# A two-stream ConvLSTM on one core: the gate product of the even pixels on GpSimd, the residual on VectorE, one row's normalisation on ScalarE

## The chip, the core and the metric

The kernel runs on one core of a Trainium2 chip. The number that counts is the device time of one execution in microseconds; the kernel before has a median of 2023.89 us over three runs (2023.4 to 2026.16). Engines are named as in the profile: PE is TensorE (its weight loads are PEld), DVE is VectorE, ACT is ScalarE, POOL is GpSimd, SP is the engine that issues the DMAs.

## What is computed

`x` is 8 images of 96 channels, 128 rows and 128 columns, float32. It is normalised in 32 groups of channels, then a recurrent cell runs down the rows, and its hidden state is added to `x`:

```python
def step(carry, row_in):                      # one row of all 8 images
    h, c = carry
    ss = conv1d(h, W_ss, padding=1)           # 96 -> 384 channels, 3 taps along the row
    gates = ss + row_in                       # row_in: 1x3 masked convolution of the normalised row
    f, i, o = (sigmoid(part) for part in ...) # each 96 channels
    g = tanh(...)
    c_new = f * c + i * g
    h_new = o * tanh(c_new)
    return (h_new, c_new), h_new
_, hs = lax.scan(step, (h0, c0), rows_of(conv(group_norm(x), W_is * mask)))
return x + hs
```

The scan has 128 steps, and each needs the hidden row of the one before.

## The kernel before

**Two streams.** The images are split in two groups of four, `s = 0` and `s = 1`. Each has its own recurrence, and the kernel alternates between them: a *half-step* n is one row of one group (`row, s = divmod(n, 2)`), 256 half-steps in all. While one group's gates are worked on by ACT and DVE, PE makes the products of the other.

**A fast convolution.** The columns are split in even and odd pixels (`t = 0` and `t = 1`, 256 columns each for four images). For a half-step the operands are `vs` (sum of the even and odd hidden pixels), `vf` (their difference) and `vd` (two shifted differences), and the same three kinds of the normalised input in `xs` for the channels that have 128 partitions free. `hx` holds the hidden row on partitions 0 to 95 and 32 normalised input channels on partitions 96 to 127. Each of the three output tiles A, B and C (one PSUM bank each: A holds the gate f, B the gate i, C the gate o, and a third of g each) gets these products, by the letters that the kernel uses:

- `P`, `Q`, `E`: the input alone (`xs`), one product each, with a `+` in the order for the next half-step;
- `1` (from `vs`) and `2` (from `vf`), into halves 0 and 1 of the bank; then `cp` (ACT copies half 0 to SBUF and adds the bias, line 508), `lo` (DVE, line 512: half 0 = copy + half 1) and `hi` (DVE, line 516: half 1 = copy - half 1);
- `0` and `3` (from `vd`), added to halves 0 and 1 afterwards, which completes the gates.

**Two row halves on PE.** Every product of 128 rows is cut into two of 64 rows, one on the upper and one on the lower half of the PE array (`Lanes`, line 372), and the halves are handed out alternately, so that two products run side by side. A half-step has 3 x 3 input products and 3 x 4 x 2 halves of the others, 33 products; each shows as two weight loads and two matmuls in the profile. Two products into the same bank from different row halves may not run at once: `mm` (line 432) puts a wait ahead of such a product, for the last product into that bank on the other half.

**The order** is written out by hand in `PERIOD` (line 678), a string of about 80 names that is emitted for each half-step n from 2 on, for all engines at once; each engine then runs its own instructions in that order, and a semaphore wait stands where an operand comes from elsewhere. A `'` means half-step n-1, `''` means n-2, `+` means n+1. Other names of the string: `ta` tanh and `si` sigmoid on ACT (lines 520, 527), `fg` f*c on DVE (532), `gt` i*g on DVE (537), `ce` the new cell (547), `th` its tanh on ACT (552), `ou` the hidden row on DVE (560), `S` the sum `vs` (573) and `F` the difference `vf` (585) on DVE, `D` the `vd` on POOL (589), `re` the residual `x += h` on POOL (607). `a` and `b` behind a name are the even and the odd pixels alone.

**Work on POOL for later rows.** Input rows come in blocks of four (`R = 4`). For the block ahead, POOL normalises one image of 128 partitions into `xw` (`widen`, line 297), makes its total (line 315) and its differences (line 316) into `xs`, and normalises the 32 shared channels of an image straight into `hx` (line 297 too). `W` in the order calls `prepare(n - 1)`, which emits all of one half-step's share; `work(n)` (line 640) lists it, `SHARED` says which image's shared channels belong to which row, and `FIRST` holds the shares of half-steps 0 to 7, which also have to catch up. `normalised` makes `total` wait for the last shared normalisation.

Before the recurrence the statistics of all images are taken while `x` streams in; the last few lines of the kernel finish half-step 255 by image pairs.

Neither `vd` nor the residual may start at will: `shifted` makes POOL wait until DVE is done with `vs` and `vf`, because these two read two SBUF operands.

Of the kernel before, what the change touches and what calls it, by code (L numbers as in the profile page):

```python
# [21 lines left out]
def kernel(  # L22
# [276 lines left out]
    def widen(engine, xw, i, n, s, k, j, lo, step=1):  # L299


        norm(
            engine,
            strided(xw[:, i, :], 0, [(step * (W + 1), n), (J + 1, 2), (1, J)]),
            (x0[:, 0, j] if s == 1 and k == lo == 0 else xr[s][:, j, lo * W : (lo + n) * W])
            .rearrange("p (r j t) -> p r t j", r=n, t=2),
            0,
            1,
            s * BH + j,
        )  # L310

    def combine(xw, n, total, differences):

        e, o = xw[:, 0:n, 0:J], xw[:, 0:n, J + 1 :]
        nc.gpsimd.tensor_add(total, e, o)  # L315
        nc.gpsimd.tensor_sub(  # L316
            differences,
            strided(xw[:, 0, :], 0, [(W + 1, n), (J, 2), (1, J)]),
            strided(xw[:, 0, :], J + 1, [(W + 1, n), (0, 2), (1, J)]),
        )  # L320

# [16 lines left out]
    normalised = {}  # L338

    def normalise_shared(engine, s, k, j, lo, hi):  # L340

        normalised[s, k] = norm(
# [61 lines left out]

    lanes = Lanes()
    whole = slice(0, P)

    class HalfStep:


        def __init__(self, n):
            self.n, (self.row, self.s) = n, divmod(n, NH)
            self.ps, self.m1, self.moving, self.done, self.gates, self.th = {}, {}, {}, set(), None, None
            self.started, self.images, self.halves, self.writer = set(), {}, {}, {}
            self.hx = hx[self.s][self.row // R % 2][:, self.row % R]
            self.xs = xs[self.s][self.row // R % 2][:, self.row % R]
            self.c = cs[self.s].rearrange("p t b j -> p (t b j)")
# [105 lines left out]
        def sigmoid(self, a):  # L523
            if self.row == 0 and a == 0:
                return
            gate = self.ps[a][0:C]
            nc.scalar.activation(gate, gate, AF.Sigmoid)  # L527
# [6 lines left out]
        def gated(self, lo=0, hi=BH, t=None):  # L534
            to = self.g if self.row > 0 else self.c
            to, i, g = (self.part(ap, lo, hi, t) for ap in (to, self.ps[1][0:C], self.g))
            nc.vector.tensor_mul(to, i, g)  # L537
# [33 lines left out]
        def total(self, engine=nc.vector, lo=0, hi=BH):  # L571
            e, o = self.pair(lo, hi)
            self.last = engine.tensor_add(self.operand("vs")[:, 0, lo:hi], e, o)  # L573
            row, s = divmod(self.n + 1, NH)
            if engine is nc.vector and row >= R and row % R < 2 and (s, row // R) in normalised:
                tc.add_manual_dep(
                    self.last.ins,
                    normalised[s, row // R].ins.name,
                    mybir.DependencyInfo(mybir.DependencyClass.Sync, mybir.DependencyReason.DATA),
                    reason="the next difference finds the next rows of x normalised",  # L580
                )
# [5 lines left out]
        def shifted(self, lo=0, hi=BH):  # L587
# [6 lines left out]
            if self.last.ins.engine != E.Pool:  # L594
                tc.add_manual_dep(
                    diff.ins,
                    self.last.ins.name,
                    mybir.DependencyInfo(
                        mybir.DependencyClass.Sync, mybir.DependencyReason.SCHED_ONLY
                    ),  # L600
                    reason="GpSimd starts when VectorE is done with both SBUF reads",
                )

        def residual(self):
            s, row = self.s, self.row
            xo = xt[s, row // R][0:C, :, row % R, :].rearrange("p b (j t) -> p t b j", t=2)
            (nc.gpsimd if 2 * row + s < last else nc.vector).tensor_add(xo, xo, self.h)  # L607
# [12 lines left out]
    def own(s, *images):  # L620
        return [(own_image, s, 1, j) for j in images]

    def shared(s, k, *images):
        return [
            (normalise_shared, nc.gpsimd, s, k, *(j if isinstance(j, tuple) else (j, 0, R)))
            for j in images
        ]

    FIRST = [
        own(0, 0),  # L630
        own(0, 1),
        own(0, 2) + shared(0, 1, 0, 1),
        own(0, 3) + [(load_rows, 0, 2)] + shared(0, 1, 2, 3),
        own(1, 0, 1),
        own(1, 2) + shared(1, 1, 0, 1),
        own(1, 3) + [(load_rows, 1, 2)] + shared(1, 1, 2, 3),
        [(own_image, 0, 2, 0), (own_image, 1, 2, 0)],
    ]

    def work(n):  # L640
# [4 lines left out]
        parts = []  # L645
        if r == R - 1 and k + 2 < NB:
            parts.append((own_image, s, k + 2, 0))
        elif r < R - 1 and k + 1 < NB:
            parts.append((own_image, s, k + 1, r + 1))
        if k + 1 < NB:  # L650
            parts += shared(s, k + 1, *SHARED[r])
        if r == R - 2 and k + 2 < NB:
            parts.append((load_rows, s, k + 2))
        return parts

    worked = set()

    def prepare(n):
        if n not in worked:
            worked.add(n)  # L660
            for part, *args in work(n):
                part(*args)

    def finish(n):
# [338 lines left out]
```

## Time and profile before

| | |
|---|---|
| median of three runs | 2023.89 us (2023.4, 2023.89, 2026.16) |
| the profiled execution | 2027.04 us, its span 2025.2 us, clock 0.997 |
| first `fg` of the hand-written order (line 532) | starts at 153.75 us |
| one half-step from there on (66 matmuls) | 7.33 us |
| data moved | 183.90 MB read, 50.33 MB written, 116 GB/s over the span |

How to read it. The span is that of the profiled execution; the 1.8 us between it and that execution's time lie outside the trace. After the statistics, the same 7.33 us pattern repeats some 250 times, so one half-step is read closely and multiplied. In the stretch from 300 to 1900 us these were the groups of one half-step apart from the matmuls (mean duration of one, from the groups by shape in that stretch; "per half-step" is the count over 218, the number of half-steps there):

| line | engine, operation | shape | per half-step | mean ns |
|---|---|---|---|---|
| 508 | ACT copy with bias (`cp`) | 128x256 | 3 | 474 |
| 520 | ACT tanh (`ta`) | 32x512 / 32x256 | 2 / 2 | 592 / 369 |
| 527 | ACT sigmoid (`si`) | 96x512 | 3 | 577 |
| 552 | ACT tanh of the cell (`th`) | 96x256 | 2 | 411 |
| 512, 516 | DVE `lo`, `hi` | 128x256 | 3, 3 | 425, 422 |
| 532 | DVE `fg` | 96x512 | 1 | 696 |
| 537, 547, 560 | DVE `gt`, `ce`, `ou` | 96x256 | 2, 2, 2 | 412, 410, 412 |
| 573, 585 | DVE `vs`, `vf` | 128x256 | 1, 1 | 418, 426 |
| 589 | POOL `vd` | 128x512 | 1 | 1041 |
| 607 | POOL residual | 96x512 | 1 | 1298 |
| 297 | POOL `xw` | 128x512 | 1 | 816 |
| 315, 316 | POOL total, differences of the own image | 128x256, 128x512 | 1, 1 | 641, 1068 |
| 297 | POOL shared channels | 32x512 (or 384, 128) | 1 to 2 | 814 (696, 465) |

In that stretch DVE was busy for 1227.2 us of 1600, ACT for 1202.3 and POOL for 1235.2.

### The profile page before, as it was taken

To read this page: it belongs to the slowest core of one execution; us is meant where nothing else is said; L and a number is where in the kernel's file an instruction comes from. 1 tells how busy PE (TensorE), PEld (TensorE's weight loads), DVE (VectorE), ACT (ScalarE), POOL (GpSimd) and SP (SyncE) were. 2 spreads that over 40 slices of the span, in tenths; PEclk is the share of its full clock that TensorE was granted. 3 is DMA by queue.
4 is the path that set the end of the run, shared out by engine and by line. 5 is a ranking of instruction groups with operands and counts; after the bars stand their busy time and mean duration, and the time that the engine had idled before them with its cause. 6 is when DMAs were issued, how large, how long until landed. Compare 5 with 4: busy or idle time off the path is not lost.

```text
span 2025.2 us, 44842 instructions
## 1 busy us (share of the span) xinstructions
PE 1923.3 (95%) x16936; PEld 1831.0 (90%) x16936; DVE 1529.1 (76%) x3996; ACT 1494.9 (74%) x3161; POOL 1473.1 (73%) x1712
## 2 busy tenths in 40 slices
PE   0289999999999999999999999999999999999998
PEld 0178999999999999999999999999999999999997
DVE  5767777777777777777777777777777777777776
ACT  3776777777777777777777777777777777777776
POOL 3348777777777777777777777777777777777752
PEclk9989999999999999999999999999999999999999
DMA  9994333444334334433433443343344333434411
GB/s 374 424 310 100 98 103 91 112 115 104 82 89 113 92 101 115 113 83 82 110 95 95 116 116 95 79 100 96 93 116 116 96 82 96 107 92 106 116 33 32
DMA packets 103382, 237.11 MB, mean 117 GB/s; under 512 B 5952, under 2 KB 8896, under 8 KB 97280
## 3 DMA queue, kind: packets, MB, share of 16 engines
q1 hardware_dynamic: 103168, 234.25, 42.0%
q8 instruction: 135, 2.21, 0.5%
q14 instruction: 79, 0.65, 0.1%
HBM read 183.90 MB, written 50.33 MB: 116 GB/s over the span
## 4 chain that ended last, share of the span: by engine, by line
PE 93%; DMA 4%; ACT 2%; DVE 1%; issue 0%; SPq 0%; POOL 0%; DVEq 0%; POOLq 0%
PE ps L442 92%; DMA piece<-in_x_dram 3%; DMA xs<-in_x_dram 1%; ACT piece L216 1%; PE ps L174 0%; ACT piece L217 0%; DVE bst L876 0%; ACT hx L295 0%; ACT piece L295 0%; DVE hx L560 0%; ACT xs L216 0%; ACT xs L217 0%; SPq L864 0%; PE pv L251 0%; DVE ps L516 0%
## 5 line engine op out<-in xcount | busy, mean ns | idle before, releaser
L442 PE MATMUL ps<-vd,wl 64*128 64x256 f32 (+1 forms) x6096 | 1390.9, 379 | 0.3
L442 PEld LDWEIGHTS ps<-vd,wl 64*128 64x128 f32 (+1 forms) x6096 | 1028.4, 186 | 45.7 <-issue 2.4
L442 PE MATMUL ps<-vs,wm 64*128 64x256 f32 (+1 forms) x3052 | 775.1, 380 | 4.9 <-POOL vs L573 4.4
L442 PE MATMUL ps<-vf,wm 64*128 64x256 f32 (+1 forms) x3052 | 766.3, 377 | 0.0
L527 ACT ACTIVATE ps<-ps 96x512 f32<-96x512 f32 x766 | 441.6, 577 | 356.2 <-PE ps L442 348.1
L442 PE MATMUL ps<-xs,wx 64*128 64x256 f32 x3080 | 637.8, 377 | 11.1 <-POOL xs L315 11.1
L589 POOL TENSOR_TENSOR vd<-hx 128x512 f32<-128x512 f32 x257 | 266.7, 1038 | 388.5 <-PE ps L442 384.8
L442 PEld LDWEIGHTS ps<-xs,wx 64*128 64x128 f32 x3080 | 494.0, 187 | 14.2 <-POOL xs L315 11.6
L520 ACT ACTIVATE g<-ps 32x256 f32<-32x256 f32 (+1 forms) x1021 | 468.6, 482 | 26.7 <-PE ps L442 6.3
L442 PEld LDWEIGHTS ps<-vf,wm 64*128 64x128 f32 (+1 forms) x3052 | 475.4, 187 | 11.0 <-PE ps L442 0.4
L442 PEld LDWEIGHTS ps<-vs,wm 64*128 64x128 f32 (+1 forms) x3052 | 459.6, 186 | 21.6 <-POOL vs L573 5.4
L512 DVE TENSOR_TENSOR ps<-m,ps 128x256 f32<-128x256 f32 x768 | 326.0, 425 | 192.5 <-ACT m L508 182.0
L442 PE MATMUL ps<-xs,wt 64*128 64x256 f32 x1530 | 453.2, 377 | 0.6 <-DVE ps L516 0.6
L508 ACT ACTIVATE m<-ps,wl 128x256 f32<-128x256 f32 x766 | 361.6, 474 | 90.9 <-PE ps L442 84.3
L532 DVE TENSOR_TENSOR ps<-ps,c 96x512 f32<-96x512 f32 x254 | 176.8, 696 | 232.9 <-PE ps L442 226.9
L607 POOL TENSOR_TENSOR x<-x,hx 96x512 f32<-96x512 f32 x255 | 330.8, 1297 | 6.7 <-DVE hx L560 6.7
L516 DVE TENSOR_TENSOR ps<-m,ps 128x256 f32<-128x256 f32 x768 | 300.8, 422 | 1.3 <-PE ps L442 1.2
L442 PEld LDWEIGHTS ps<-xs,wt 64*128 64x128 f32 x1530 | 280.0, 186 | 12.8 <-DVE ps L516 1.0
L316 POOL TENSOR_TENSOR xs<-xw 128x512 f32<-128x512 f32 (+1 forms) x254 | 270.9, 1067 | 0.0
L297 POOL TENSOR_SCALAR hx<-x,rstd,nmr 32x384 f32<-32x384 f32 (+2 forms) x312 | 225.8, 724 | 33.2 <-DMA x<-in_x_dram 1.1
L297 POOL TENSOR_SCALAR xw<-xr,rstd,nmr 128x512 f32<-128x512 f32 x252 | 205.6, 816 | 7.1 <-DVE nmr L289 6.5
L537 DVE TENSOR_TENSOR g<-ps,g 96x256 f32<-96x256 f32 x507 | 189.0, 413 | 3.8 <-ACT g L520 3.8
(91 smaller groups left out, 1223.1 us busy)
## 6 DMA issues: line engine op xcount, KB each, us to landing
xr<-in_x_dram SPq DMA_DIRECT2D x124, 512.0 KB, 6.4
x<-in_x_dram SPq DMA_DIRECT2D x63, 768.0 KB, 6.1
out_dram<-x SPq DMA_DIRECT2D x62, 768.0 KB, 4.6
xs<-in_x_dram SPq DMA_DIRECT2D x30, 1024.0 KB, 12.3
piece<-in_x_dram SPq DMA_DIRECT2D x16, 1024.0 KB, 12.3
x<-in_x_dram SPq DMA_DIRECT2D x62, 256.0 KB, 3.2
xs<-in_x_dram SPq DMA_DIRECT2D x4, 512.0 KB, 8.7
out_dram<-x SPq DMA_DIRECT2D x2, 576.0 KB, 3.7
```

The source lines that it names most:

```text
L297: return engine.tensor_scalar(dst, src, scale, shift, ALU.mult, ALU.add)
L316: nc.gpsimd.tensor_sub(differences, strided(xw[:, 0, :], 0, [(W + 1, n), (J, 2), (1, J)]), strided(xw[:, 0, :], J + 1, [(W + 1, n), (0, 2) ...
L442: made = nc.tensor.matmul(self.ps[a][:, bass.ts(half, HB)][:, cols], weights[rows, bass.ts(a, P)], rhs[rows, cols], start=new, stop=False, ...
L508: nc.scalar.activation(self.m1[a], m1, AF.Identity, bias=column)
L512: nc.vector.tensor_add(self.ps[a][:, 0:HB], self.m1[a], self.ps[a][:, HB:])
L516: nc.vector.tensor_sub(hi, self.m1[a], hi)
L520: nc.scalar.activation(self.part(g, lo, hi, t), self.part(ps, lo, hi, t), AF.Tanh)
L527: nc.scalar.activation(gate, gate, AF.Sigmoid)
L532: nc.vector.tensor_mul(f, f, self.c)
L537: nc.vector.tensor_mul(to, i, g)
L589: diff = nc.gpsimd.tensor_sub(self.operand("vd", 2)[:, :, lo:hi], strided(h, 1, [(BH * JP - 1, 2), (JP, hi - lo), (1, J)]), strided(h, 0, ...
L607: (nc.gpsimd if 2 * row + s < last else nc.vector).tensor_add(xo, xo, self.h)
```

## The change

The parts, all of which come with a new hand-written order:

- The product i*g of the even pixels (`gta`) goes to POOL. [...] the sigmoid of the gate i is cut in two: the odd pixels stay in PSUM (`siBb`), and the even ones are written to a new SBUF tile `i` (`siBa`).
- The residual goes from POOL to DVE, from half-step 2 on; the next POOL instruction of the prepared work waits for it (`hold`).
- The three pieces of the own image are emitted one by one (`W1`, `W2`, `W3`), with the even product between `W1` and `W2`; the shared channels (`U`) are emitted one half-step later than before. Image 3's first row of each block is normalised on ACT (`X`), and the wait of `total` for `normalised` is gone.
- `FIRST` is spread out: fewer own images in one half-step, some shared images on ACT, three pieces put off to half-steps 9, 11 and 13.
- In `PERIOD`, the products `3` now come ahead of `0` for A and B and both later than before, the gate tiles A and B of a half-step end earlier in the order, `vs` comes ahead of `vf`, and `Q` of tile B is made two half-steps ahead (`QB*`).

```diff
-    def combine(xw, n, total, differences):
-        e, o = xw[:, 0:n, 0:J], xw[:, 0:n, J + 1 :]
-        nc.gpsimd.tensor_add(total, e, o)
+    def add_pixels(xw, n, total):
+        nc.gpsimd.tensor_add(total, xw[:, 0:n, 0:J], xw[:, 0:n, J + 1 :])
+    def subtract_pixels(xw, n, differences):
         nc.gpsimd.tensor_sub(
...
+    def hold(made, until):
+        if until.ins.engine != E.Pool:
+            tc.add_manual_dep(made.ins, until.ins.name,
...
+                reason="GpSimd starts when VectorE is done with both SBUF reads",
...
-        def sigmoid(self, a):
+        def sigmoid(self, a, lo=0, hi=BH, t=None):
...
-            gate = self.ps[a][0:C]
-            nc.scalar.activation(gate, gate, AF.Sigmoid)
+            gate = self.part(self.ps[a][0:C], lo, hi, t)
+            if t == 0 and self.n > NH:
+                self.even_input = self.tile("i", (C, HB))
+                to = self.even_input.rearrange("p (b j) -> p b j", b=BH)
+            else:
+                to = gate
+            nc.scalar.activation(to, gate, AF.Sigmoid)
...
-            nc.vector.tensor_mul(to, i, g)
+            if t == 0 and self.even_input is not None:
+                i = self.even_input.rearrange("p (b j) -> p b j", b=BH)
+                nc.gpsimd.tensor_mul(to, i, g)
+            else:
+                nc.vector.tensor_mul(to, i, g)
...
-            if engine is nc.vector and row >= R and row % R < 2 and (s, row // R) in normalised:
-                tc.add_manual_dep(
...
-            (nc.gpsimd if 2 * row + s < last else nc.vector).tensor_add(xo, xo, self.h)
+            if self.n < NH:
+                nc.gpsimd.tensor_add(xo, xo, self.h)
+            else:
+                residuals.append(nc.vector.tensor_add(xo, xo, self.h))
...
+    def own(s, k, j, buffer=0):
+        to, wide = xs[s][k % 2], xw[buffer]
+        return (
+            (widen, nc.gpsimd, wide, 0, R, s, k, j, 0),
+            (add_pixels, wide, R, to[:, :, 0, j, :]),
+            (subtract_pixels, wide, R, to[:, :, 1:3, j, :]),
+        )
...
-            (normalise_shared, nc.gpsimd, s, k, *(j if isinstance(j, tuple) else (j, 0, R)))
+            (normalise_shared, nc.scalar if hi == 1 else engine, s, k, j, lo, hi)
...
+    spread = own(1, 1, 0, 1)
     FIRST = [
-        own(0, 0),
-        own(0, 1),
-        own(0, 2) + shared(0, 1, 0, 1),
-        own(0, 3) + [(load_rows, 0, 2)] + shared(0, 1, 2, 3),
-        own(1, 0, 1),
-        own(1, 2) + shared(1, 1, 0, 1),
-        own(1, 3) + [(load_rows, 1, 2)] + shared(1, 1, 2, 3),
-        [(own_image, 0, 2, 0), (own_image, 1, 2, 0)],
+        ([], own(0, 1, 0), []),
+        (shared(0, 1, 0), own(0, 1, 1), []),
+        (beside(0, 1, 1) + shared(0, 1, 2), own(0, 1, 2), []),
+        (beside(0, 1, 3) + shared(1, 1, 0), own(0, 1, 3), [spread[0], (load_rows, 0, 2)]),
+        (beside(1, 1, 1) + shared(1, 1, 2), own(1, 1, 1), [spread[1]]),
+        (shared(1, 1, 3), own(1, 1, 2), [spread[2]]),
+        ([], own(1, 1, 3), [(load_rows, 1, 2)]),
+        ([], own(0, 2, 0), []),
     ]
+    LATER = dict(zip((9, 11, 13), own(1, 2, 0, 1)))
...
+        for part, *args in now:
+            made = part(*args)
+            if made is not None and made.ins.engine == E.Pool and residuals:
+                hold(made, residuals[-1])
+                residuals.clear()
...
     PERIOD = (
-        "2A hiC' siA' D'' 1B 1A taA' 2B fg' 3C' 1A 0C' re'' taB' 2A 2B EC' 1B cpA 0C' 2C W loA cpB "
-        "3C' 1C siB' loB PB+ QA+ hiA taCb' 2C hiB taCa' 0A gtb' 1C siC' gta' EA 0B ceb' cpC 3A PA+ "
-        "cea' thb' PC+ 3B loC tha' QC+ oub' EB oua' QB+ 3A F' 3B 0A S' 0B"
+        "1A hiC' D'' siBb' 1B 2A siBa' 2B 0C' siA' 2A re'' 3C' taB' 1A 1B fg' W1 0C' 2B cpA 3C' "
+        "2C loA cpB U EC' 1C loB PB+ PA+ taCa' hiA 1C taCb' QA+ hiB gta' 2C siC' gtb' 3A 3B W2 EA "
+        "ceb' cpC EB cea' 0A thb' W3 loC 0B tha' PC+ oub' 0A oua' 3B 3A S' 0B QB* F' X taA QC+"
     )
-    SPLIT = ("taC", "gt", "ce", "th", "ou")
+    SPLIT = ("taC", "siB", "gt", "ce", "th", "ou")
...
-            if name == "W":
-                prepare(n - 1)
+            if name in "UX":
+                if n >= NH:
+                    prepare(n - NH, name)
+                continue
+            if name[0] == "W":
+                prepare(n - 1 + name.count("+") - name.count("'"), name.strip("W+'"))
```

More of the change, by code (lines that the diff above doesn't have):

```diff
@@ L299, in widen @@
     def widen(engine, xw, i, n, s, k, j, lo, step=1):
-        norm(
+        return norm(
             engine,
@@ L320, in combine @@
         )
+    def combine(xw, n, total, differences):
+        add_pixels(xw, n, total)
+        subtract_pixels(xw, n, differences)
     def own_image(s, k, j):
@@ L336, in own_row @@
         )
-    normalised = {}
     def normalise_shared(engine, s, k, j, lo, hi):
-        normalised[s, k] = norm(
+        return norm(
             engine,
@@ L403, in wait @@
                 self.waited = number
+    def hold(made, until):
+        if until.ins.engine != E.Pool:
+            tc.add_manual_dep(
+                made.ins,
+                until.ins.name,
+                mybir.DependencyInfo(
+                    mybir.DependencyClass.Sync, mybir.DependencyReason.SCHED_ONLY
+                ),
+                reason="GpSimd starts when VectorE is done with both SBUF reads",
+            )
+    residuals = []
     lanes = Lanes()
@@ L414, in __init__ @@
             self.started, self.images, self.halves, self.writer = set(), {}, {}, {}
+            self.even_input = self.last = None
             self.hx = hx[self.s][self.row // R % 2][:, self.row % R]
@@ L573, in total @@
             self.last = engine.tensor_add(self.operand("vs")[:, 0, lo:hi], e, o)
-            row, s = divmod(self.n + 1, NH)
-            if engine is nc.vector and row >= R and row % R < 2 and (s, row // R) in normalised:
-                tc.add_manual_dep(
[L577 to L581, printed above, removed]
         def difference(self, engine=nc.vector, lo=0, hi=BH):
@@ L593, in shifted @@
             )
[L594 to L602, printed above, removed]
+            hold(diff, self.last)
         def residual(self):
@@ L618, with shared, beside @@
     SHARED = (((0, 0, R), (3, 0, 1)), ((1, 0, R),), ((2, 0, R),), ((3, 1, R),))
-    def own(s, *images):
-        return [(own_image, s, 1, j) for j in images]
-    def shared(s, k, *images):
+    def own(s, k, j, buffer=0):
[4 more added lines that the diff above has]
+            (subtract_pixels, wide, R, to[:, :, 1:3, j, :]),
+        )
+    def shared(s, k, *images, engine=nc.gpsimd):
+        parts = [j if isinstance(j, tuple) else (j, 0, R) for j in images]
         return [
-            (normalise_shared, nc.gpsimd, s, k, *(j if isinstance(j, tuple) else (j, 0, R)))
-            for j in images
-        ]
+            (normalise_shared, nc.scalar if hi == 1 else engine, s, k, j, lo, hi)
+            for j, lo, hi in parts
+        ]
+    def beside(s, k, *images):
+        return shared(s, k, *images, engine=nc.scalar)
+    spread = own(1, 1, 0, 1)
     FIRST = [
-        own(0, 0),
-        own(0, 1),
-        own(0, 2) + shared(0, 1, 0, 1),
-        own(0, 3) + [(load_rows, 0, 2)] + shared(0, 1, 2, 3),
-        own(1, 0, 1),
-        own(1, 2) + shared(1, 1, 0, 1),
-        own(1, 3) + [(load_rows, 1, 2)] + shared(1, 1, 2, 3),
-        [(own_image, 0, 2, 0), (own_image, 1, 2, 0)],
+        ([], own(0, 1, 0), []),
[6 more added lines that the diff above has]
+        ([], own(0, 2, 0), []),
     ]
+    LATER = dict(zip((9, 11, 13), own(1, 2, 0, 1)))
     def work(n):
@@ L644, in work, with prepare @@
         k, r = divmod(row, R)
[L645 to L662, printed above, removed]
+        ahead, image = (k + 2, 0) if r == R - 1 else (k + 1, r + 1)
+        return (
+            shared(s, k + 1, *SHARED[r]) if k + 1 < NB else [],
+            own(s, ahead, image) if ahead < NB else (),
+            ([(load_rows, s, k + 2)] if r == R - 2 and k + 2 < NB else [])
+            + ([LATER[n]] if n in LATER else []),
+        )
+    worked = {}
+    def prepare(n, which="123"):
+        channels, image, rest = worked.setdefault(n, [list(parts) for parts in work(n)])
+        now = []
+        for name, engine in (("X", nc.scalar), ("U", nc.gpsimd)):
+            if name in which:
+                now += [part for part in channels if part[1] is engine]
+                channels[:] = [part for part in channels if part[1] is not engine]
+        for i in "123":
+            if i in which and int(i) <= len(image) and image[int(i) - 1]:
+                now.append(image[int(i) - 1])
+                image[int(i) - 1] = None
+        if image.count(None) == len(image) and n not in closed:
+            closed.add(n)
+            now += rest
+        for part, *args in now:
[3 more added lines that the diff above has]
+                residuals.clear()
+    closed = set()
     def finish(n):
```

## The prediction

> **What bounds the kernel now.** I read the shares of the engines and the chain of waits first, then the stretch from 300 to 1900 us, then the order of time of one half-step, engine by engine.
>
> ```profile
> PE 1923.3 (95%) x16936; PEld 1831.0 (90%) x16936; DVE 1529.1 (76%) x3996; ACT 1494.9 (74%) x3161; POOL 1473.1 (73%) x1712
> ...
> PE 93%; DMA 4%; ACT 2%; DVE 1%; issue 0%; SPq 0%; POOL 0%; DVEq 0%; POOLq 0%
> ...
> 300.00:1900.00 1600.00, 1600.00 (x14398) 1537.23 (x14396) 1227.20 (x3272) 1202.27 (x2619) 1235.21 (x1364) 1.00 0.39 99
> ```
>
> PE is the chain, and no other engine is above 77% in the steady stretch. 66 matmuls in 1600/14398 us each make a half-step of 7.334 us. But a busy PE is not yet a full one: matmul ends are modelled. The weight loads tell more.
>
> ```profile
> 806.72 0.44 PEld L442 LDWEIGHTS ps<-xs,wx 64*128 64x128 f32 x4
> 807.20 0.36 PEld L442 LDWEIGHTS ps<-vf,wm 64*128 64x128 f32 x2
> 807.69 0.18 PEld L442 LDWEIGHTS ps<-vd,wl 64*128 64x128 f32 x1
> ...
> 807.37 0.59 PE L442 MATMUL ps<-vf,wm 64*128 64x256 f32 x2
> 807.72 0.45 PE L442 MATMUL ps<-vd,wl 64*128 64x256 f32 x1
> ...
> 806.35 0.90 DVE L512 TENSOR_TENSOR ps<-m,ps 128x256 f32<-128x256 f32 x2 [0.70 <-ACT m L508]
> 807.15 0.75 DVE L516 TENSOR_TENSOR ps<-m,ps 128x256 f32<-128x256 f32 x2
> ```
>
> Within one row half, one instruction follows another every 0.216 us (loads at 805.64, 805.86, 806.08, 806.29, 806.51, 806.72). A product is two of them, two row halves run side by side, so a product costs 0.216 and 33 of them 7.13. The half-step has 7.334: 0.21 is missing. All loads of the half-step stand on this raster but one: the `vd` load at 807.69, which its row half could have begun at about 807.20. It is the first of 0A. The first `hi` (line 516) ran from 807.15 to 807.57, and the load follows 0.12 later. The late row half loses some 0.39, the other 0.03: (0.39+0.03)/2 = 0.21. So the bound is PE, with one bubble a half-step where 0A waits for `hi` of A.
>
> **What the Trainium skill says.** "TensorE: Matmul & The Clock Gate", LDWEIGHTS, prices a load at its columns over 1.2 GHz, 107 ns for 128; the late load agrees: its matmul is listed at 807.72 but takes 0.45 instead of 0.38, so its data begin near 807.80, 0.11 after the load. "SBUF — State Buffer", Who interferes with whom, says that a VectorE instruction with two SBUF inputs and a GpSimd one that reads SBUF exclude each other, the later waiting out the earlier. The trace agrees near its start:
>
> ```profile
> 160.46 1.34 POOL L316 TENSOR_TENSOR xs<-xw 128x512 f32<-128x512 f32 x1
> 160.79 1.29 DVE L573 TENSOR_TENSOR vs<-hx 128x256 f32<-128x256 f32 x1
> ...
> 2021.12 0.69 DVE L607 TENSOR_TENSOR x<-x,hx 96x512 f32<-96x512 f32 x1
> ...
> 803.85 1.04 POOL L589 TENSOR_TENSOR vd<-hx 128x512 f32<-128x512 f32 x1 [1.03 <-PE ps L442]
> ...
> 810.25 0.42 DVE L585 TENSOR_TENSOR vf<-hx 128x256 f32<-128x256 f32 x1
> 810.59 0.42 DVE L573 TENSOR_TENSOR vs<-hx 128x256 f32<-128x256 f32 x1
> ...
> 812.28 0.70 DVE L532 TENSOR_TENSOR ps<-ps,c 96x512 f32<-96x512 f32 x1 [0.93 <-PE ps L442]
> ```
>
> `vs` took 1.29 instead of 0.42 and ended 0.28 after POOL's instruction (160.46 + 1.34). The other lines give the prices of a residual on DVE (0.69) and the order of `vf`, `vs` and `vd`, and the idle 0.93 of DVE ahead of `fg`.
>
> **The new order on PE.** I number the 33 products from the first one that needs the new `vs` (slot 0); slot k starts near 0.216 k. Before, 0A is slot 18. In the new order the first product that waits for `hi` is 3A in slot 20, 3B is slot 21; tiles A and B have their first products in slots 7 and 10, and C is complete in slot 13, as before. `hi` of A ended 4.05 after slot 0 before, 3A can begin at 4.05+0.12+0.11 = 4.28, and slot 20 is at 4.31. The bubble goes, with 0.03 to spare.
>
> What is late next: the waits between the row halves. Two products of one bank on different halves may not overlap. From a product's start to the earliest start of one that waits for it: 0.59 (the two matmuls of `vf` above), 0.06 until the load and 0.11 of load:
>
> ```profile
> 803.91 0.63 PE L442 MATMUL ps<-vs,wm 64*128 64x256 f32 x4
> ...
> 804.60 0.18 PEld L442 LDWEIGHTS ps<-vs,wm 64*128 64x128 f32 x1
> ```
>
> (the four end at 804.54). That is 0.76. Such waits reach back three slots. Let odd slots lag even ones by d: an odd slot lies 0.432+d after the third one before it, an even one 0.864-d. An odd wait costs nothing from d = 0.33 up, an even one up to d = 0.10. Before, the waits of this kind stand at slots 5, 9, 17 and 30, odd ones and then an even one, and the bubble at 18 makes the turn between for free. In the new order they stand at 5, 9, 17, 27 (0A behind 0A in 24) and 28 (3B behind 0B in 25). Between 27 and 28 the even half must lose 0.33-0.10 = 0.23, once in each half-step (33 is odd, so the halves then change roles and d is 0.33 again). Half of it counts: 0.11. New half-step: 7.13+0.11 = 7.24, or 0.10 less than before.
>
> **Can the other engines follow in 7.24?** Times after slot 0.
> - ACT: A' is complete at -0.27, B' at 0.05. tanh A' -0.23 to 0.36, `siBb`, `siBa` (not in this trace: the two tanh shapes differ by 0.22 for 256 elements, so 0.58-0.22 = 0.36; written to SBUF between that and the 0.41 of line 552; I take 0.36 and 0.41), sigmoid A' to 1.64, tanh B' to 2.2; the copies start at 2.25 and 2.79 as before. +0.2 of ACT time, in its idle 1.38.
> - DVE: one `gt` less (-0.41), the residual +0.69. `vd` starts on POOL 0.17 after `vf`, the residual could 0.26 after it (the `hi` of C stands between), so it waits for `vd` and ends about 0.55 after that: 1.83. Then `fg` until 2.5; the second `lo` waits for ACT until 3.29 and the first needs 0.43 ahead of it, so some 0.35 of waiting hide this. If POOL should wait instead, `vd` ends at 2.1 and is needed at 4.3.
> - The hidden row: both `hi` end at 4.05 and 4.38, `gtb` 4.29-4.70, `ceb` (+0.04 for its own input) 4.75-5.16, `cea` from 5.08, `loC`, `oub` 5.74, `oua` 6.07-6.48, `vs` 6.52-6.95. Slot 0 needs it 0.16 earlier than 7.24, at 7.08: 0.13 to spare. `vf` is needed two slots later. Before, `vf` came first and two `gt` stood in this row.
> - POOL: `vd` 0.24-1.28, `xw` held by the residual 2.0-2.8, shared 2.9-3.7, the even product (two SBUF inputs, 256 elements, as line 315: 0.64; below, 2.6 cycles an element at 1.2 GHz by the skill's "GPSIMD Engine Reference", Performance versus the Vector engine, 0.55 with nothing fixed; above, half the old residual's 1.30 and 0.2 fixed, 0.85) from 4.0, when tanh C' is there, to 4.66 (`cea` takes it at 5.08), total to 5.26, differences to 6.28; `vs` begins at 6.52. Busy 5.0 instead of 5.67.
> - Image 3's first row on ACT (32x128: 0.27 by the tanh's slope, 0.47 as the copy with a bias) comes once in eight half-steps, when ACT is idle. The banks that `PA+`, `PC+` and `QB*` need are read for the last time over 0.5 us earlier. The shared channels come one half-step later, which the loads only gain from; SP's stores now wait for DVE, 0.8 earlier than for POOL.
>
> **The sum.** Some 246 half-steps at -0.10 make -25. At the start, `fg` before (lines 532) began at 153.75, 163.03, 172.27, 180.22, 187.78, 195.23, 202.69 and 210.80: 5.7 over seven of 7.334, because POOL had two own images or two shared ones in a half-step. Spreading saves between 0 and 5; I take 3. At the end the residual of half-step 254 stands on DVE ahead of the last cell: +0.7. -25-3+0.7 = -27.5, 2027.0 to 1999.5 in the profiled execution, and as that lies 3.1 above the median of its kernel, 1996 as a median.
>
> **Rivals.** A change under 0.2% (4 us) can't be told from none here.
> 1. *The row halves' wait costs nothing*, since the trace shows no late one and the loads might be drawn ahead. Then the floor of 7.13 decides, which the hidden row just permits (6.95+0.16 = 7.11): 246 x 0.207 = 51, with the start 1970. Against it: a wait at distance three did hold the load at 804.60 until its product had ended.
> 2. *A thin margin breaks*: 3A has 0.03, the hidden row 0.13. ACT late by 0.1, or `siBa` at its upper end, gives 7.30 or so: 246 x 0.035 = 9, about 2012; at the worst the old bubble is back and only the start is gained.
> 3. *Slower: POOL's differences still run when `vs` begins.* Place: end of each half-step, price as at 160.79, up to 0.87 on the way to slot 0. It decides once POOL is over 0.25 late, which an even product of 0.9, or a `vd` drawn out by the residual, would give. In the early half-steps before, with such meetings, `fg` came every 7.45 to 7.57: at 7.46, +0.125 x 246 = 31, less 3: 2052. For it: DVE and POOL now meet in each half-step. Against: once late, POOL's ring (`vd`, hold, five pieces, then `vs`) closes in about 6.9, under 7.24, so it catches up.
>
> **Chances.** The forecast 0.60 (own range 1989 to 2003), first rival 0.13, second 0.14, third 0.13. Of the second, some 0.03 lies within 0.2%. Faster 0.84, same 0.03, slower 0.13. The range takes in the first rival and most of the second: 1968 to 2014.
>
> **What would show it.** A half-step of 7.24 between the `fg` of DVE; no `vd` load of 3A off the raster; one late load at 3B, late by 0.2, in alternating row halves; residuals on DVE that last near 1.6 with a start right behind `hi`, and `vs` at 0.42. If `vs` lasts over 0.5, the third rival is right; if loads stand on the raster throughout, the first; if 3A's load follows `hi` by 0.12, the second.

## The result and the profile after

The changed kernel takes 1997.16 us in the median of four runs (1996.7 to 1999.4), beside 2023.64 us for the kernel before in the same session (2023.2 to 2026.16). The ratio is 0.987, with a 95% interval of 0.985 to 0.989. The profiled execution took 1999.4 us, its span 1997.6 us, at a clock of 0.996. The forecast was 1996.

First the page of the changed kernel: the busy shares and the chain of waits. Below the dots stands the stretch from 300 to 1900 us; its columns are window, length, and then PE, PEld, DVE, ACT and POOL busy time with the number of instructions, clock, DMA share, GB/s.

```profile
PE 1895.7 (95%) x16936; PEld 1840.8 (92%) x16936; DVE 1799.4 (90%) x3997; ACT 1566.6 (78%) x3477; POOL 1303.4 (65%) x1648
...
PE 93%; DMA 4%; ACT 2%; DVE 1%; issue 0%; SPq 0%; POOL 0%; DVEq 0%; POOLq 0%; ACTq 0%
...
300.00:1900.00 1600.00, 1600.00 (x14611) 1569.91 (x14609) 1482.26 (x3322) 1281.31 (x2933) 1106.37 (x1328) 1.00 0.40 102
```

The chain is PE's as before. 66 matmuls in 1600/14611 us each make a half-step of 7.227 us, 0.107 less than 7.334. VectorE is busy for 93% of this stretch (1482.26 of 1600), where it was at 77%. That looks like a new bound. The run with a 34th product below shows that it is not one. Some 170 us of it are residuals that stand and wait (222 times 1.45 less 0.69, see the next lines).

The new groups of that stretch are these, by shape; the columns are group, busy time and mean ns of one, idle time ahead of it and what ended it.

```profile
L621 DVE TENSOR_TENSOR x<-x,hx 96x512 f32<-96x512 f32 x222 | 322.3, 1452 | 0.0
...
L562 POOL TENSOR_TENSOR g<-i,g 96x256 f32<-96x256 f32 x221 | 160.7, 727 | 80.3 <-ACT g L538 80.3
...
L600 DVE TENSOR_TENSOR vs<-hx 128x256 f32<-128x256 f32 x222 | 94.5, 426 | 7.7
...
L550 ACT ACTIVATE i<-ps 96x256 f32<-96x256 f32 x222 | 84.5, 381 | 7.0
L550 ACT ACTIVATE ps<-ps 96x256 f32<-96x256 f32 x222 | 80.2, 361 | 5.4
L295 ACT ACTIVATE hx<-x,nmr,rstd 32x128 f32<-32x128 f32 x56 | 27.6, 492 | 1.5
```

The residual is listed at 1.45 us, though one with nothing beside it took 0.69 before: it runs into `vd` on GpSimd in nearly every half-step. `vs` lasts 0.426, so GpSimd does not hold it.

Here is one half-step of the two engines in order of time. Slot 0, the first product that needs the new `vs`, begins at 800.36.

```profile
800.66 1.48 DVE L621 TENSOR_TENSOR x<-x,hx 96x512 f32<-96x512 f32 x1
802.07 0.68 DVE L555 TENSOR_TENSOR ps<-ps,c 96x512 f32<-96x512 f32 x1
803.15 0.93 DVE L530 TENSOR_TENSOR ps<-m,ps 128x256 f32<-128x256 f32 x2 [0.40 <-ACT m L526]
803.99 0.75 DVE L534 TENSOR_TENSOR ps<-m,ps 128x256 f32<-128x256 f32 x2
...
806.88 0.42 DVE L600 TENSOR_TENSOR vs<-hx 128x256 f32<-128x256 f32 x1
...
800.56 1.04 POOL L608 TENSOR_TENSOR vd<-hx 128x512 f32<-128x512 f32 x1 [1.07 <-PE ps L460]
...
804.36 0.73 POOL L562 TENSOR_TENSOR g<-i,g 96x256 f32<-96x256 f32 x1 [0.27 <-ACT g L538]
...
805.65 1.07 POOL L318 TENSOR_TENSOR xs<-xw 128x512 f32<-128x512 f32 x1
```

The residual begins right behind the last `hi` and ends 0.54 after `vd` (802.14 and 801.60). DVE still has 0.40 to wait before the first `lo`, so the residual costs nothing. GpSimd's differences end at 806.72, and `vs` begins at 806.88.

Last the loads and matmuls on PE. *Raster* stands for the even step of 0.216 us at which one row half takes its loads and matmuls. The first lines are those of slot 20, 3A, which now is the first product that waits for `hi`; the others are those about the one place where PE stumbles, slots 25 to 28. Each line is a load or a matmul, or several of one name in a row.

```profile
804.25 0.19 PEld L460 LDWEIGHTS ps<-xs,wx 64*128 64x128 f32 x1
804.53 0.18 PEld L460 LDWEIGHTS ps<-vd,wl 64*128 64x128 f32 x1
...
804.68 0.38 PE L460 MATMUL ps<-vd,wl 64*128 64x256 f32 x1
...
805.76 0.19 PEld L460 LDWEIGHTS ps<-xs,wx 64*128 64x128 f32 x1
805.86 0.19 PEld L460 LDWEIGHTS ps<-vd,wl 64*128 64x128 f32 x1
805.97 0.19 PEld L460 LDWEIGHTS ps<-xs,wx 64*128 64x128 f32 x1
806.19 0.18 PEld L460 LDWEIGHTS ps<-vd,wl 64*128 64x128 f32 x1
...
806.51 0.41 PEld L460 LDWEIGHTS ps<-vd,wl 64*128 64x128 f32 x4
...
805.97 0.38 PE L460 MATMUL ps<-xs,wx 64*128 64x256 f32 x1
806.08 0.38 PE L460 MATMUL ps<-vd,wl 64*128 64x256 f32 x1
806.19 0.38 PE L460 MATMUL ps<-xs,wx 64*128 64x256 f32 x1
```

The load of 3A comes 0.12 after the end of the first `hi` (803.99 + 0.42 = 804.41), and that is 0.07 behind the raster (804.25 + 0.216). Its matmul all the same starts on the raster, at 804.68, one step behind the matmul before it on this half (804.46). No time is lost there, but the margin is some 0.04 us: the load could have stood 0.11 behind the raster, as the next place shows.

The `xs` loads (PC, slot 26) belong to one row half and follow each other by 0.216 (805.76, 805.97). That half could load 3B, slot 28, at 806.19; the `vd` load that stands there is 0A's, slot 27, on the other half. 3B's load comes at 806.51 instead: the last matmul of 0B in slot 25, on the other half, is listed from 806.08 to 806.46. So the load comes 0.05 after 0B's end, and the data of 3B 0.11 later, at 806.62. Of this 0.32 the half loses only 0.21. A load on the raster starts a whole step of 0.216 ahead of its matmul (805.76 and 805.97), where the late one needs 0.11, so 0.11 of being late is covered. "TensorE: Matmul & The Clock Gate", Step-by-step: what each phase is for, in the Trainium skill, says that PE draws loads ahead of running matmuls where the row groups don't conflict, or where the load goes to the background weight buffer. The trace agrees that loads run ahead: the second `xs` load starts at 805.97, together with the first `xs` matmul of its own half, which by the page would be the second case. A load that waits for the other half loses that lead. In the next half-step the same thing happens in the other row half: between 300 and 1900 us, 222 products start 0.21 late, one in each half-step, and no other product does.

### The profile page after: what moved, and what is told of

Same layout as the page of the kernel before. It is cut to its first block, busy times and chain, and to the rows that moved or that the text cites. A ratio compares the mean times of both kernels' runs of the same rounds, so it can differ in the third digit from the quotient of the medians.

```text
span 1997.6 us, 45563 instructions
## 1 busy us (share of the span) xinstructions
PE 1895.7 (95%) x16936; PEld 1840.8 (92%) x16936; DVE 1799.4 (90%) x3997; ACT 1566.6 (78%) x3477; POOL 1303.4 (65%) x1648
## 4 chain that ended last, share of the span: by engine, by line
PE 93%; DMA 4%; ACT 2%; DVE 1%; issue 0%; SPq 0%; POOL 0%; DVEq 0%; POOLq 0%; ACTq 0%
PE ps L460 92%; DMA piece<-in_x_dram 3%; DMA xs<-in_x_dram 1%; PE ps L174 1%; ACT piece L216 1%; ACT piece L217 0%; DVE bst L920 0%; ACT g L538 0%; ACT hx L295 0%; ACT piece L295 0%; ACT xs L216 0%; ACT xs L217 0%; ACT ps L550 0%; SPq L908 0%; DVE hx L587 0%
## 5 line engine op out<-in xcount | busy, mean ns | idle before, releaser
L460 PE MATMUL ps<-vd,wl 64*128 64x256 f32 (+1 forms) x6096 | 1275.6, 380 | 0.4
L460 PEld LDWEIGHTS ps<-vd,wl 64*128 64x128 f32 (+1 forms) x6096 | 943.6, 186 | 25.7 <-issue 1.5
L460 PE MATMUL ps<-vs,wm 64*128 64x256 f32 (+1 forms) x3052 | 714.3, 377 | 4.7 <-POOL vs L600 4.3
L460 PEld LDWEIGHTS ps<-vf,wm 64*128 64x128 f32 (+1 forms) x3052 | 527.9, 187 | 9.8 <-issue 0.8
L550 ACT ACTIVATE ps<-ps 96x512 f32<-96x512 f32 x767 | 388.8, 507 | 14.4
L460 PE MATMUL ps<-xs,wt 64*128 64x256 f32 x1530 | 384.8, 377 | 0.4 <-DVE ps L534 0.4
L621 DVE TENSOR_TENSOR x<-x,hx 96x512 f32<-96x512 f32 x254 | 366.5, 1443 | 0.0
L562 POOL TENSOR_TENSOR g<-i,g 96x256 f32<-96x256 f32 x252 | 183.2, 727 | 110.9 <-ACT g L538 110.8
L297 POOL TENSOR_SCALAR hx<-x,rstd,nmr 32x512 f32<-32x512 f32 (+1 forms) x249 | 195.4, 785 | 26.6 <-DVE x L621 2.2
L574 DVE TENSOR_TENSOR c<-ps,g 96x256 f32<-96x256 f32 x508 | 190.6, 415 | 8.7
```

The lines of the kernel that those rows point to most:

```text
L297: return engine.tensor_scalar(dst, src, scale, shift, ALU.mult, ALU.add)
L460: made = nc.tensor.matmul(self.ps[a][:, bass.ts(half, HB)][:, cols], weights[rows, bass.ts(a, P)], rhs[rows, cols], start=new, stop=False, ...
L550: nc.scalar.activation(to, gate, AF.Sigmoid)
L562: nc.gpsimd.tensor_mul(to, i, g)
L574: nc.vector.tensor_add(c, f, g)
L621: residuals.append(nc.vector.tensor_add(xo, xo, self.h))
```

## The experiments

Every run is the changed kernel with the edit shown. The time of before in the same sessions was 2023.8 to 2024.4 us.

**3B two slots later.** PE's late load stands at 3B. Is it the pair 0B, 3B, or something that the half-step owes in any case? (One row half runs a fixed time behind the other. A wait over three slots is free or not by which half lags; where that has to change, one half falls back. This is the *turn* below.)

```diff
-PC+ oub' 0A oua' 3B 3A S' 0B QB* F' X taA QC+
+PC+ oub' 0A oua' QC+ 3A S' 3B QB* F' X taA 0B
```

> The changed kernel with product 3B moved two slots later, five behind 0B, so that the late load at 3B has no reason left in that place. Theory 1 (a half-step has 33 products, so the two row halves change roles from one half-step to the next, and what is in step in one is out of step in the other): the one late load of 0.21 us per pair of half-steps does not vanish but shows up at another place, in the other parity; half-step 7.23 us, time 1997 (1990 to 2004). Theory 2 (the late load belongs to the pair 0B, 3B alone): it goes; half-step 7.13, time about 1972. Theory 3 (VectorE, 93% busy in the steady part, sets the pace): no change, 1997, and the matmuls show a wait for VectorE instead.

It took 1997.81 us (ratio to before 0.987, 0.986 to 0.989), with half-steps of 7.227 again. In the order of time the load of 3B is on the raster now, and the late one stands at slot 5, the second product 2A:

```profile
806.27 0.51 PEld L460 LDWEIGHTS ps<-vf,wm 64*128 64x128 f32 x4
806.70 0.40 PEld L460 LDWEIGHTS ps<-vd,wl 64*128 64x128 f32 x2
807.13 0.18 PEld L460 LDWEIGHTS ps<-vf,wm 64*128 64x128 f32 x1
807.13 0.18 PEld L460 LDWEIGHTS ps<-vd,wl 64*128 64x128 f32 x1
```

The four `vf` loads alternate between the halves; the last one, of the odd half, starts at 806.59, so that half could load at 806.81. It loads at 807.13, late by 0.32 as 3B was. The loss moves and does not go: the pair is not the cause. VectorE as the pace-setter is not excluded by the time alone, but the place of the late load and the next runs speak against it.

**A 34th product in each half-step.** PC is made twice, which leaves the result as it is. In one kernel all waits that reach back three slots stand in odd slots, in the other 3B stays three behind 0B, in an even one.

```diff
-PC+ oub' 0A oua' 3B 3A S' 0B QB* F' X taA QC+
+PC+ oub' 0A oua' ZC+ 3A S' 3B QC+ F' X taA 0B QB*      (one parity)
+PC+ oub' 0A oua' 3B 3A S' 0B ZC+ QB* F' X taA QC+      (both parities)
...
+            if part == "Z":
+                step.started.discard(order[tile_])
+                step.piece("P", order[tile_])
+                continue
```

> The changed kernel with a 34th product in each half-step (the first product of bank C, PC, made twice, which leaves the result as it is), placed so that 3B lies five slots behind 0B, as in the run with 3B moved. Now all waits that reach back three slots stand in odd slots, and 34 being even the row halves keep their roles. Theory (the 0.21 missing per half of 33 products is the turn of the roles): no late load at all, half-step 34 x 0.216 = 7.34 us, so the 34th product costs 0.117 and not 0.216; time 1997 + 246 x 0.117 = 2026 (2022 to 2032). Rival (the lost time has another cause and stays): 7.227 + 0.216 = 7.44, time 2050.

> The changed kernel with the same 34th product at another place (slot 31, between 0B and QB), and 3B left in slot 28, three behind 0B. The roles are kept, but one wait stands in an even slot and four in odd ones, so the halves have to turn twice in each half-step. Theory: two late loads of 0.21 us in each half-step, one per half, 7.34 + 0.21 = 7.55 us, time 1997 + 246 x 0.327 = 2077 (2068 to 2086), though the number of products is that of the other run with 34. Rival (an even number of products alone does away with the loss): 7.34, 2026.

They took 2023.95 us (2022.9 to 2025.64) and 2075.97 us (2075.41 to 2076.5). The same stretch, first with one parity, then with both:

```profile
300.00:1900.00 1600.00, 1600.00 (x14829) 1569.48 (x14828) 1460.15 (x3272) 1265.46 (x2888) 1086.65 (x1309) 1.00 0.40 100
```

```profile
300.00:1900.00 1600.00, 1600.00 (x14414) 1565.05 (x14412) 1419.12 (x3179) 1230.76 (x2808) 1056.86 (x1272) 1.00 0.39 98
```

A half-step has 68 matmuls here: 1600/14829 x 68 = 7.337 and 1600/14414 x 68 = 7.548. The first is 34 x 0.216 = 7.34 with no late load, so this product costs 0.110 and not 0.216, and with PE's raster full VectorE can't be what sets the pace. The second has the same products and two late loads in each half-step, at slots 5 and 28. In the first, no product starts late between 300 and 1900 us. So what is lost in 33 products is the turn: the halves change roles because 33 is odd, and a wait over three slots is free in one parity alone.

**A wait over one slot.** 3B's second product directly behind 0B, to price such a wait by itself.

```diff
-0B tha' PC+ oub' 0A oua' 3B 3A
+0B tha' 3B oub' 0A oua' PC+ 3A
```

> The changed kernel with product 3B put directly behind 0B, on whose end it waits across the row halves, and PC moved to where 3B was. Theory (a wait across the row halves costs 0.76 us from the earlier product's last matmul to the later one's first, less the distance between them): the halves lose about 0.65 us at even and 0.36 us at odd half-steps, half-step about 7.63, time about 2095 (2060 to 2120). Rival (such waits are hidden by the queue, VectorE sets the pace): no change, 1997.

2103.32 us (ratio 1.039, 1.037 to 1.041), half-steps of 1600/13788 x 66 = 7.659, where 7.63 was expected. The loss over 33 x 0.216 = 7.13 is 0.53, expected 0.50. The rival falls: neither the queue nor VectorE hides it.

**The order and the places, one without the other.** In the first run the gate product goes back to VectorE; in the second the residual goes back too; in the third the order is that of before, and the three pieces of work stay at their new places. In all three the sigmoid of the gate i stays cut in two.

```diff
-            if t == 0 and self.n > NH:                      (first and second)
+            if t == 0 and self.n > last:
...
-            if self.n < NH:                                 (second)
+            if self.n < last:
```

> The changed kernel with the even pixels' gate product back on VectorE, all else kept. Theory (the new order needs the hidden row at its slot, and VectorE reaches it about 0.3 us later with a second product of 0.4 us in front): the load of hidden becomes the late one in every half-step, half-step 7.4 to 7.5 us, time about 2049 (2030 to 2065), slower than the kernel before. Rival (the product only fills VectorE's idle time, the new order alone makes the gain): 1997 to 2005.

> The new order and the image-3 row on ScalarE, with both the gate product and the residual at their old places. Theory (the order removes the late load at product A, but only with VectorE freed ahead of the hidden row): half-step about 7.44, time about 2050 (2025 to 2070), slower than the kernel before. Rival (the order alone makes the gain): about 1997.

2056.98 us (ratio 1.016, 1.015 to 1.018) and 2056.09 us (1.016, 1.014 to 1.017), half-steps of 7.474 and 7.473. In the order of time of the first, the first load with the new `vs` comes 0.05 after VectorE has written it (803.72 + 0.43), and before it the loads pause:

```profile
803.72 0.43 DVE L600 TENSOR_TENSOR vs<-hx 128x256 f32<-128x256 f32 x1
...
803.60 0.51 PEld L460 LDWEIGHTS ps<-xs,wx 64*128 64x128 f32 x3
804.20 0.34 PEld L460 LDWEIGHTS ps<-vs,wm 64*128 64x128 f32 x4
...
805.39 0.18 PEld L460 LDWEIGHTS ps<-vf,wm 64*128 64x128 f32 x1
```

From the first `hi` (800.43) to `vs` it takes 3.29 us here, against 2.89 in the changed kernel (803.99 to 806.88). The one product of 0.41 is the difference. The expectation spoke of the load of hidden; the late one is that of `vs` in slot 0, the first that reads the new hidden row, and behind it the roles turn a second time (slot 5, the load at 805.39). The size is 60 us, 52 expected. The starts of the matmuls split it: over the 214 half-steps from 300 to 1900 us one row half loses 0.24 in the mean at `vs` and one 0.24 at slot 5, beside the 0.21 at 3B, so each of the two has about half of what is new. No product loses time at 3A in either run: the new order alone does away with the old bubble, and pays for it with these two.

```diff
-1A hiC' D'' siBb' 1B 2A siBa' 2B 0C' siA' 2A re'' 3C' taB' 1A 1B fg' W1 0C' 2B ... 3A 3B W2 EA ...
+2A hiC' siA' D'' 1B 1A taA' 2B fg' 3C' 1A 0C' re'' taB' ... 1C siBb' siBa' loB ... 0A gta' gtb' ...
```

> The changed kernel with the order of before on every engine, but the gate product of the even pixels, the residual and image 3's row at their new places. Theory (the copies on ScalarE and not VectorE set when hidden A is ready, so freeing VectorE doesn't remove the late load at product A in slot 18): half-step 7.30 to 7.36 us, time 2015 to 2030, like before. Rival (the freed VectorE brings the gain, the order is of no account): about 1997.

2064.64 us (ratio 1.020, 1.018 to 1.021), half-steps of 7.48: slower than before by 40, and both theories miss the time. In this order the sigmoid of the gate i stands between the copies and tanh of C on ScalarE. In two halves it takes longer, tanh C comes later, and the product on GpSimd follows it:

```profile
803.50 0.37 ACT L550 ACTIVATE ps<-ps 96x256 f32<-96x256 f32 x1
803.89 0.38 ACT L550 ACTIVATE i<-ps 96x256 f32<-96x256 f32 x1
804.30 0.65 ACT L538 ACTIVATE g<-ps 32x256 f32<-32x256 f32 x2
...
805.03 0.72 POOL L562 TENSOR_TENSOR g<-i,g 96x256 f32<-96x256 f32 x1 [0.30 <-ACT g L538]
...
805.78 0.42 DVE L574 TENSOR_TENSOR c<-ps,g 96x256 f32<-96x256 f32 x1 [0.20 <-POOL g L562]
...
803.97 0.75 DVE L534 TENSOR_TENSOR ps<-m,ps 128x256 f32<-128x256 f32 x2
804.50 0.18 PEld L460 LDWEIGHTS ps<-vd,wl 64*128 64x128 f32 x1 [0.19 <-issue]
...
807.23 0.42 DVE L604 TENSOR_TENSOR vf<-hx 128x256 f32<-128x256 f32 x1
807.71 0.29 PEld L460 LDWEIGHTS ps<-vf,wm 64*128 64x128 f32 x2
```

The even half of the new cell waits for GpSimd, 0.29 behind the place that it would have right after the odd half (805.16 + 0.33, the step from one to the other where neither waits). The hidden row comes late behind it: the first load of `vf` follows 0.06 after `vf` is written (807.71 for 807.65), and the two row halves lose 0.15 there and 0.09 at `vs`, which makes 0.12 a half-step of the 0.15 that this kernel is slower. In the kernel before no product started late at these two. That GpSimd's wait is the whole reason for this was not tested. The old bubble is still there, as the theory had it: the load of 0A at 804.50 comes 0.11 after the end of the first `hi` (803.97 + 0.42). In the changed kernel both halves of that sigmoid run at the front of the half-step, and the cell has no such wait. So each half of the change alone costs: 2057 for the order without the product moved, 2065 for the places without the order, 1997 with both. They are one change.

**The residual, the row, and both back on GpSimd.**

```diff
-            if self.n < NH:                                                       (residual)
+            if self.n < last:
...
-            (normalise_shared, nc.scalar if hi == 1 else engine, s, k, j, lo, hi)  (row)
+            (normalise_shared, engine, s, k, j, lo, hi)
```

> The changed kernel with the residual additions back on GpSimd, the gate product staying there too. Theory (GpSimd then has all of the old work and the new product in one half-step and ends about when the shifted row is to be written): VectorE's shifted copy is held by GpSimd in part of the half-steps; half-step 7.23 to 7.30, time 1997 to 2014. Rival 1 (moving the residual was without effect): 1997. Rival 2 (GpSimd is over full and sets the pace): half-step above 7.5, over 2060.

> The changed kernel with image 3's first row normalised on GpSimd again instead of ScalarE. Theory (two of every eight half-steps get about 0.46 us more on GpSimd, whose differences end only 0.16 us before the shifted row is written): the shifted row is late by up to 0.2 us in 62 half-steps, time 0 to 12 us longer, 1997 to 2009. Rival 1 (ScalarE's row of 0.49 us delays something there): time shorter by 1 to 5 us. Rival 2 (more than one such half-step in a row runs over): over 2015.

> The changed kernel with both the residual and image 3's row back on GpSimd, so that of the three moved parts only the gate product stays moved, under the new order. Each of the two alone cost 0 to 4 us. Theory (the gate product and the order are the gain, but GpSimd, whose differences with the residual alone already end 0.1 us into the shifted row, gets 0.46 us more in two of eight half-steps): the shifted or summed row is late by 0.3 to 0.5 us there, 62 x 0.4 x 0.5 to 1 = 12 to 25 us over the kernel with the residual back: 2012 to 2026. Rival (GpSimd catches up within the half-step and the shifted row is never held): 2001, as with the residual back alone.

With the residual back 2001.55 us (ratio 0.989, 0.987 to 0.990), with the row back 1997.77 (0.987, 0.985 to 0.988), with both back 2027.14 (1.001, 1.001 to 1.002). Half-steps are 7.229, 7.229 and 7.345. The first two costs are within the expected ranges, at or near their lower ends, but not by the mechanism that was expected: in neither run does `vs` or `vf` last over 0.43 between 300 and 1900 us. Of the residual's 4.4 us the profiled runs show 2.3 between the first and the last `fg`; the rest is not located. For the third the size is just above the range and the mechanism is another one: `vs` is never held. These are the waits of that kernel from 300 to 1900 us (who waited for whom, us in total, times, longest) and one place in its order of time:

```profile
DVE c L574 <- POOL g L562: 27.2, 54, 0.8
...
805.57 1.38 POOL L297 TENSOR_SCALAR hx<-x,rstd,nmr 32x512 f32<-32x512 f32 x2
807.02 0.72 POOL L562 TENSOR_TENSOR g<-i,g 96x256 f32<-96x256 f32 x1
...
808.30 1.06 POOL L318 TENSOR_TENSOR xs<-xw 128x512 f32<-128x512 f32 x1
...
807.78 0.42 DVE L574 TENSOR_TENSOR c<-ps,g 96x256 f32<-96x256 f32 x1 [0.56 <-POOL g L562]
...
809.23 0.42 DVE L600 TENSOR_TENSOR vs<-hx 128x256 f32<-128x256 f32 x1
```

Two shared normalisations (1.38) and the residual together push the gate product back until the new cell waits 0.56 for it, in two of eight half-steps, and the hidden row with it. By the starts of `fg` these two last 7.65 and 7.74: 0.42 + 0.51 over 7.23, in some 28 blocks of eight 26 us. From the first `fg` to the last this kernel takes 27.9 longer than the one with the residual back alone; the medians differ by 25.6. So the residual and the row are two covers for the same margin on GpSimd. Either may go back at little or no cost; both may not.

**The start.** The residual of half-step 1 on VectorE as well.

```diff
-            if self.n < NH:
+            if self.n < 1:
```

> The changed kernel with the residual of half-step 1 on VectorE too (the change leaves those of half-steps 0 and 1 on GpSimd). Theory (my sum took 3 us for the start where about 1 came, because in the first half-step of the hand-written order GpSimd has this residual and two own images, which run into the shifted and summed rows): the first interval between two forget products falls from 10.56 us to 9.3 or so, the later ones stay; time about 1996, 1.2 less. Rival (the loads of the rows set the start): the first interval stays at 10.5.

1997.04 us (ratio 0.987, 0.985 to 0.988). The interval between the first two `fg` falls from 10.56 to 9.59, the next one grows from 7.48 to 7.77. In the order of time of the changed kernel the two rows that are held in that interval are

```profile
160.17 0.64 POOL L314 TENSOR_TENSOR xs<-xw 128x256 f32<-128x256 f32 x1
160.18 0.91 DVE L600 TENSOR_TENSOR vs<-hx 128x256 f32<-128x256 f32 x1
160.77 1.25 POOL L318 TENSOR_TENSOR xs<-xw 128x512 f32<-128x512 f32 x1
161.01 1.28 DVE L604 TENSOR_TENSOR vf<-hx 128x256 f32<-128x256 f32 x1
```

With this edit `vf` lasts 0.41 there and `vs` 0.99. The place is right. What comes out, 0.7 us where 1.2 was expected, is too little for the medians to show.

**All waits five slots apart.** If the turn comes from waits that reach back three slots, an order without them should reach 7.13.

```diff
-... 0C' siA' 2A ... 0C' 2B cpA 3C' 2C loA cpB U EC' 1C loB PB+ PA+ taCa' hiA 1C taCb' QA+ hiB gta' 2C ...
+... 0C' siA' QC ... 2A 2B cpA 0C' 2C loA cpB U 3C' EC' 1C loB PA+ EA taCa' hiA QA+ taCb' EB hiB gta' 1C ...
```

> The changed kernel with an order of the same 33 products in which every wait across the row halves reaches back five slots or more (the second product 2A, 0C, 1C and 2C two slots later, QC of the same half-step at slot 5, EA, EB, PA, QA, PB and EC moved into the places that come free). Theory (those waits, three slots back, are all that is missing to 7.13): the raster has no late load but perhaps EB, which follows its operand by 0.07 us too early; half-step 7.13 to 7.17 us, time 1973 to 1984. Rival 1 (the hidden row is the next bound, its floor is 7.11): half-step 7.15 to 7.25 with the loads of vs late. Rival 2 (a half-step of 33 products loses a turn whatever the distances, or VectorE at 93% sets the pace): 7.23, time 1997.

2147.74 us (ratio 1.061, 1.059 to 1.063), half-steps of 7.84, which no theory had. To space the products I had put EA and EB ahead of `hi` of their banks, and then `hi` waits for them: in its waits from 300 to 1900 us stands

```profile
DVE ps L534 <- PE ps L460: 85.9, 204, 0.4
```

which the changed kernel doesn't have, and the load of 3A is late again. So this run prices that placement and tells nothing of the turn. Whether an order of 33 products without the turn exists is open: with EA and EB behind `hi`, I found none that still completes A and B in time.

No run was faster than the changed kernel by more than the runs scatter. Three parts of the change were not taken back alone: the new `FIRST`, `QB*`, and the dropped wait of `total`.

## Why the prediction was right

| step of the prediction | predicted | measured |
|---|---|---|
| steady half-step | 7.24 us | 7.227 us |
| its share of the sum | 246 x -0.10 = -25 us | 253 x -0.107 = -27.1 us |
| start | -3 us (0 to 5) | -0.6 us |
| end | +0.7 us | +0.2 us |
| profiled execution | -27.5 us | 2027.04 to 1999.4: -27.6 us |

The 253 are the intervals between the starts of `fg` in the order that is written out. Start and end are what lies outside them or goes beyond the steady gain in the first twelve and the last.

- **The bubble at `hi` goes.** 3A's matmul is on the raster, with some 0.04 us to spare where 0.03 was forecast. Its load does follow `hi` by 0.12, which the prediction had named as the sign of its second rival; the sign was no good, because a load can be 0.11 late at no cost. The order alone takes this bubble away, and with the places alone it stays. But with the order alone the hidden row is late, so the gain takes the moved product too.
- **The turn at 3B.** Right in place, in its alternation and in size: 0.21 for 0.23. The 0.76 us between a product and one that waits for it on the other half is 0.75 in the trace (0B's first matmul, one raster step ahead of the one at 806.08, to 806.62). Moving 3B, the 34th product and the near wait each gave the time that this price asks for; rival 1, that such waits are free, is out.
- **The timetable.** From slot 0, `vs` was put at 6.52 to 6.95; it ran from 6.52 to 6.94. The residual was to end at 1.83 and ended at 1.78. The first copy was put at 2.25 "as before", but before it started at 2.32 (805.84, slot 0 at 803.52); it ran at 2.28, and nothing hung on it.
- **The even product was mis-sized:** 0.64 taken, 0.727 measured, inside the bounds. The low end of these, from the 2.6 cycles of the Trainium skill's "GPSIMD Engine Reference", Performance versus the Vector engine, was too low for this shape. It cost nothing, as the cell takes the product only at 5.08 and it is there at 4.73.
- **Image 3's row on ScalarE:** 0.49 us, just above my 0.27 to 0.47, and free, as supposed.
- **The start was the mis-sized term of the sum:** 3 us taken, 0.6 measured. Of these only 0.26 can be put down to the change: so much more than the steady gain the first twelve intervals save. The other 0.35, a first `fg` at 153.40 for 153.75, is within the scatter: in the twelve experiments it starts between 150.40 and 153.36. I had counted that fewer own images in a half-step free GpSimd, but the first hand-written half-step still has two, with a residual ahead of them. The steady part gave 2.1 more, and the two errors cancel, so that the sum came out within 0.1 us by luck.
- **Rival 3 had the wrong place.** It saw GpSimd's last pass run into `vs`. With the residual back that pass in the median ended 0.1 after `vs` began, and half-steps stayed at 7.229. What breaks first is the gate product ahead of the cell, and only with the residual and the row both back.

## What to carry to other kernels

Where products on two row halves wait for each other, count slots and parities: a wait over three slots was free in one parity alone, and an odd number of products then paid one turn in each round, in both orders that kept such waits and had nothing else late. Move work and reorder together, and test each alone: here either half made the kernel slower by 1.6% to 2%, and two of the moved parts covered the same margin, so that taking back one of them tells almost nothing. A busy share of 93% on an engine need not be a bound; see how long its instructions last when nothing is beside them.

## What was not expected of the hardware

- Passes of VectorE and GpSimd that both read two SBUF operands held each other only beyond a short overlap. With the residual and the row back, `vs` began at 809.23 with GpSimd's differences listed until 809.36, and lasted 0.42. With the residual back alone `vs` began up to 0.15 before their listed end in 168 of 221 half-steps, and lasted 0.43 in the mean. At 160.18 it began beside a GpSimd sum of 0.64 just under way, and lasted 0.91. "SBUF — State Buffer", Who interferes with whom, in the Trainium skill, calls the ports that the two share an exclusive lock. The trace agrees for the residual (1.45 for 0.69), but not in the last 0.15 us of a listed pass. Spans on GpSimd are rough, so this may be the listing.
- A product of two SBUF operands of 96x256 takes longer on GpSimd (0.727 us) than a sum of 128x256 (0.641). The runs don't say why.
